# Seven products of halves in place of eight in the down projection of six blocks

## The chip, the cores and the metric

The kernel runs on one core of a Trainium2 chip. The time is that of the device, in microseconds (us), from start to end of one execution. One execution is also taken by the hardware profiler; the rows below come from it. Engines: PE is TensorE (matmuls; PEld is its weight load), DVE is VectorE, ACT is ScalarE, POOL is GpSimd, SP is SyncE, whose queue issues nearly all DMAs here. L74 is line 74 of the kernel, the helper through which all matmuls go, so matmuls are told apart by the names of their tiles.

## The reference

One transformer block on `x` of 4 x 1024 x 512 in float32. `x` is normalized to `xn`; a linear attention with decay (16 heads of 32, chunks of 128, ternary weights) and a gated feed-forward are both computed from `xn`, and both are added to `x`:

```python
xn = _layernorm(x)
gate = jnp.einsum('bsd,hd->bsh', xn, w_gate)      # 2048 hidden
up   = jnp.einsum('bsd,hd->bsh', xn, w_up)
gated = jax.nn.silu(gate) * up
ffn  = jnp.einsum('bsh,dh->bsd', gated, w_down)   # the down product
x = x + attention(xn, ...) + ffn
```

The change is to the last product, `gated` (tokens x 2048) by `w_down` (2048 x 512).

## The kernel before

**Blocks and stages.** The 4096 tokens are worked off in eight blocks of 512 (`b` is 0 to 7 in the code; the text counts blocks 1 to 8). The 2048 hidden units are 16 tiles `j` of 128. A block's feed-forward has two halves `hh` of eight tiles. For each tile, `ffn_up` makes the gate and up products (two stages of 12 matmuls of 512 columns into a bank `psf`), ACT applies silu (L693), DVE multiplies by the up product (L696), and the float32 result is split into two float16 tiles: ACT casts the high half (L699), POOL or DVE subtracts it for the low half (L700). Both lie in a tile `ghl`, of which there are eight. After eight tiles, `ffn_down` makes the down product: for each of four groups of 128 tokens, 8 tiles times 3 matmuls of 512 columns (high by high, high by low, low by high), 96 matmuls per half, and DVE adds the bank to `acc` (L720). `acc` holds `x` at the start and goes out by DMA when its last part is in.

**Weights.** Block 1 scales the weights by powers of two, splits them in two float16 halves and keeps them: gate and up in DRAM (`gu_d`, loaded again per block in 512 KB pieces `gu`, four buffers), down in SBUF (`wd`, all of it). In block 1 the down product follows two tiles at a time; from block 2 on it runs as above.

**Attention.** It is cut in halves of 256 tokens. `att_half` is a generator of some 27 steps: q, k (staged through DRAM into `qst` and `kst`), v, then scores into a single bank `pss`, multiplied by the mask on DVE (L545), split by ACT and POOL (L547, L548), products with v into `psa`, state, norms, and the projection (`turn`, `proj`). PSUM has three banks `psf`, four `psa`, one `pss`.

**Order.** One step of attention follows each stage of the feed-forward. The list `at` says in which step each half starts, `mh` when its input `h` is made; a block has 48 steps (32 up stages and 16 pieces of the down product), the program 384. TensorE keeps this order. The instructions of the other engines and of SP's queue are put in order by the scheduler when the program is built; each queue then runs in that order. Within an engine an instruction that waits holds up all behind it.

```python
    at = [round(36 + 22.4 * n) for n in range(2 * NB - 2)]
    at += [at[-1] + 14, at[-1] + 28]
```

Of the kernel before, what the change touches and what calls it, by code (L numbers as in the profile page):

```python
# [28 lines left out]
def block_kernel(ctx, tc, x, qkv_w, qkv_nwT, proj_w, proj_nwT, proj_nw, norm_w, s, w_gu, w_down, out):  # L29
# [73 lines left out]
    gu_d = dram.tile([P, NJ * 2048], F16, tag="gu_d", name="gu_d")  # L103
    wqkT = ct([P, CC, 2 * C], F16, "wqkT")
    wvT = ct([P, CC, C], F16, "wvT")
    wpT = ct([P, CC, C], F16, "wpT")
    wd = ct([P, NJ, 2, C], F16, "wd")
# [173 lines left out]
    raw, gu0, gq, lg = {}, {}, {}, [None]  # L281

    def raw_pair(g, kind):

        if kind == 2:
            return [t32(), t32()]
        if g == 0 and kind == 0:
            t = wt([P, 2, C], F32, "kn", 1)
            return [t[:, 0, :], t[:, 1, :], t]
        return [wt([P, C], F32, *(("ghl", 8) if g % 2 else ("xin", 4) if g else ("xn2", 2))) for _ in range(2)]  # L290
# [29 lines left out]
    def group_scale(g, kinds=(0, 1, 2)):  # L320
# [9 lines left out]
        if 0 in kinds:  # L330
            inverse(ug[:, gs], o[:, 0:1], 1 / XS)
            V.tensor_scalar(bsc0[:, gs], o[:, 0:1], 2.0**-30 / XS, None, ALU.mult)
# [9 lines left out]
    def group_conv(g, r, kinds=(0, 1, 2)):  # L342
# [3 lines left out]
        for kind in kinds:  # L346
# [3 lines left out]
            else:  # L350
                hi, lo = (wd[:, j, n, :] for n in range(2))
# [329 lines left out]
    def ffn_up(b, j, gu, bs, gts, E):  # L681
        xT = blk[b][0]
        xhi, xlo = xT[:, 0], xT[:, 1]
        pg = []
        for kind in range(2):
# [8 lines left out]
            else:  # L694
# [3 lines left out]
                ghl = wt([P, 2, HB], F16, "ghl", 8)  # L698
                A.copy(ghl[:, 0, :], gf)  # L699
                E.tensor_tensor(ghl[:, 1, :], gf, ghl[:, 0, :], ALU.subtract)  # L700
                gts.append(ghl)
            yield

    def ffn_down(b, k, js, gts, c):
        tsl = slice(k * P, (k + 1) * P)
        pd = bank(ps_f)
        for n, j in enumerate(js):
            gh, gl = gts[n][:, 0, tsl], gts[n][:, 1, tsl]
            T.matmul(pd, gh, wd[:, j, 0, :], start=(n == 0), stop=False)
            T.matmul(pd, gh, wd[:, j, 1, :], start=False, stop=False)  # L710
            T.matmul(pd, gl, wd[:, j, 0, :], start=False, stop=(n == len(js) - 1))
            if n % 4 == 3:
                if n == len(js) - 1:
                    add_acc(b * 4 + k, pd, c)
                yield
        if len(js) % 4:
            add_acc(b * 4 + k, pd, c)

    def add_acc(g, ps, c):
        V.scalar_tensor_tensor(acc[g], ps, c, acc[g], ALU.mult, ALU.add)  # L720
        parts[g] -= 1
        if parts[g] == 0:
            SY.dma_start(of[g * P : (g + 1) * P, :], acc.pop(g))

    def load_acc(b):
        for k in range(4):
            acc[4 * b + k] = load_x(4 * b + k, "acc", 8)
            parts[4 * b + k] = 1 + (2 if b else NG)

    def ffn(b):  # L730
        for hh in range(2):
            js = range(hh * NJ // 2, (hh + 1) * NJ // 2)
            gts = []
            for j in js:
                gu = wt([P, 2, 2, CC, P], F16, "gu", 4)
                SY.dma_start(gu.rearrange("p a b c d -> p (a b c d)"), gu_d[:, j * 2048 : (j + 1) * 2048])
                yield from ffn_up(b, j, gu, bsc, gts, V if j > js[-4] else G)
# [192 lines left out]
```

## Time and profile before

| | |
|---|---|
| median of 3 runs | 1368.39 us (1367.6 to 1370.64) |
| the profiled execution | 1368.61 us, its span 1366.7 us |
| granted TensorE clock, mean | 0.994 |
| busy: PE, DVE, ACT, POOL | 1322.6, 719.9, 550.3, 619.6 us |
| down matmuls (`psf<-wd,ghl`, 512 columns) | 1536, busy 352.3 us |
| gate and up matmuls (`psf<-xT,gu`, 512 columns) | 3072, busy 703.4 us |
| DMA: moved, busy share of queue 1 | 178.11 MB, 47.0% |

Busy time of a group counts only time in which no earlier matmul is still running; the mean duration of a matmul in the profile (380 ns) is longer than its spacing in a dense stream, since matmuls are pipelined. Spacing is read from start to start in the timeline. A group's row ends with the idle time of its engine ahead of it and what ended it; a row of the waits is engine, tile, line, what it waited for, us in total, times, longest.

### The profile page before, as it was taken

The page shows a single profiled execution, that of the slowest core. Times are in us where ns is not written, and L with a number is a line of the kernel's source. Part 1 is how long each engine was busy: PE and PEld are TensorE (multiplying, and loading weights), DVE is VectorE, ACT ScalarE, POOL GpSimd, SP SyncE. Part 2 cuts the span into 40 slices and gives each one's busy share as a digit, 9 for nine tenths or more (in the row PEclk, how much of TensorE's full clock was granted, in tenths as well). Part 3 has the DMA queues.
Part 4 walks back from the last instruction along what each step waited for, and adds up shares of the span by engine and source line. Part 5 has one row for each costly group of instructions (what it writes and reads, how often), then busy time and mean ns, then how long its engine had stood idle before and what let it go on. Part 6 is the DMA issues. An engine that isn't in the chain of part 4 may idle for free.

```text
span 1366.7 us, 21760 instructions
## 1 busy us (share of the span) xinstructions
PE 1322.6 (97%) x8514; PEld 695.6 (51%) x8514; DVE 719.9 (53%) x1415; ACT 550.3 (40%) x1033; POOL 619.6 (45%) x603
## 2 busy tenths in 40 slices
PE   5998989999999999999999999999999999999998
PEld 2443445554555545455455545555555555565554
DVE  7897764445544354453644446453553445356444
ACT  6754443343433334333334243342424334244341
POOL 3657672444624254353634246342545245255451
PEclk9999999999999999999999999999999999999999
DMA  9833836146261554426363354626283444535420
GB/s 343 294 124 114 231 101 180 48 137 156 87 191 31 165 128 125 140 59 173 94 155 108 103 141 104 178 69 162 80 181 95 116 116 106 142 109 124 105 66 31
DMA packets 155974, 178.11 MB, mean 130 GB/s; under 512 B 101600, under 2 KB 101600, under 8 KB 155872
## 3 DMA queue, kind: packets, MB, share of 16 engines
q1 hardware_dynamic: 155728, 176.73, 47.0%
q8 instruction: 66, 1.08, 0.3%
q14 instruction: 36, 0.29, 0.1%
q10 hardware_dynamic: 144, 0.01, 0.0%
HBM read 119.55 MB, written 33.55 MB: 112 GB/s over the span
## 4 chain that ended last, share of the span: by engine, by line
PE 79%; DVE 7%; POOL 7%; issue 3%; DMA 3%; ACT 1%; SPq 0%; POOLq 0%; ACTq 0%; DVEq 0%
PE psf L74 58%; PE psa L74 19%; PE pss L74 2%; DMA xin<-in_x_dram 2%; DMA xT<-xn 1%; POOL t L548 1%; DVE acc L720 1%; POOL xn L437 1%; DVE t L696 1%; DVE gs L312 1%; POOL rs L396 1%; POOL wd L360 1%; DVE t L239 0%; POOL ghl L700 0%; POOL gu L360 0%
## 5 line engine op out<-in xcount | busy, mean ns | idle before, releaser
L74 PE MATMUL psf<-xT,gu 128*128 128x512 f16 x3072 | 703.4, 381 | 10.6 <-POOL gu L360 5.5
L74 PEld LDWEIGHTS <-gu 128*128 128x128 f16 x3072 | 294.7, 98 | 338.0 <-issue 10.1
L74 PE MATMUL psf<-wd,ghl 128*128 128x512 f16 x1536 | 352.3, 380 | 2.7 <-ACT t L693 1.1
L74 PEld LDWEIGHTS <-ghl 128*128 128x128 f16 x1536 | 146.9, 98 | 164.3 <-issue 3.3
L548 POOL TENSOR_TENSOR t<-t,t 128x512 f16<-128x512 f32 x128 | 149.5, 1168 | 164.2 <-ACT t L547 163.9
L700 POOL TENSOR_TENSOR ghl<-t,ghl 128x512 f16<-128x512 f32 x86 | 102.6, 1193 | 163.4 <-ACT ghl L699 150.2
L696 DVE SCALAR_TENSOR_TENSOR t<-psf,bsc,t 128x512 f32<-128x512 f32 x128 | 95.9, 749 | 121.2 <-PE psf L74 104.8
L699 ACT CAST ghl<-t 128x512 f16<-128x512 f32 x128 | 79.0, 617 | 176.1 <-DVE t L696 175.6
L545 DVE SCALAR_TENSOR_TENSOR t<-pss,rs,mask 128x512 f32<-128x512 f32 x128 | 95.3, 744 | 77.2 <-PE pss L74 74.7
L693 ACT ACTIVATE t<-psf,ug 128x512 f32<-128x512 f32 x128 | 87.5, 684 | 98.0 <-PE psf L74 96.6
L74 PE MATMUL psa<-h,wqkT 128*128 128x256 f16 x1024 | 122.2, 273 | 0.0
L519 POOL TENSOR_TENSOR t<-t,t 128x512 f16<-128x512 f32 x28 | 32.6, 1163 | 195.3 <-ACT t L518 195.3
L547 ACT CAST t<-t 128x512 f16<-128x512 f32 x128 | 79.1, 618 | 101.9 <-DVE t L545 96.3
L74 PEld LDWEIGHTS <-wqkT 128*128 128x128 f16 x1024 | 99.7, 98 | 23.4
L720 DVE SCALAR_TENSOR_TENSOR acc<-psf,c,acc 128x512 f32<-128x512 f32 x56 | 41.8, 747 | 63.0 <-PE psf L74 62.7
L74 PEld LDWEIGHTS <-t 128*128 128x128 f16 x1040 | 47.6, 97 | 35.0 <-POOL t L548 3.4
L74 PE MATMUL psa<-wvT,h 128*128 128x512 f16 x256 | 60.5, 379 | 0.0
L74 PE MATMUL pss<-qst,kst 96*128 96x128 f16 x512 | 49.2, 218 | 8.7 <-DVE t L545 6.5
L74 PE MATMUL psa<-wpT,vhl 128*128 128x512 f16 x240 | 56.7, 379 | 0.0
L620 POOL TENSOR_TENSOR vhl<-t,vhl 128x512 f16<-128x512 f32 x30 | 34.7, 1155 | 48.0 <-ACT vhl L619 48.0
L573 POOL TENSOR_TENSOR t<-t,t 128x512 f32<-128x512 f32 x28 | 36.1, 1288 | 44.1 <-DVE t L572 18.6
L508 DVE SCALAR_TENSOR_TENSOR vhl<-psa,rs,vhl 128x512 f16<-128x512 f32 x32 | 24.0, 749 | 56.2 <-ACT vhl L507 54.5
(188 smaller groups left out, 1340.8 us busy)
## 6 DMA issues: line engine op xcount, KB each, us to landing
gu<-gu_d SPq DMA_DIRECT2D x112, 512.0 KB, 3.6
qst<-sd SPq DMA_DIRECT2D x48, 256.0 KB, 4.8
kst<-sd SPq DMA_DIRECT2D x48, 256.0 KB, 4.7
xin<-in_x_dram SPq DMA_DIRECT2D x32, 256.0 KB, 3.0
acc<-in_x_dram SPq DMA_DIRECT2D x32, 256.0 KB, 2.8
gu_d<-gu SPq DMA_DIRECT2D x16, 512.0 KB, 4.1
sd<-qhl SPq DMA_DIRECT2D x16, 512.0 KB, 2.6
sd<-khl SPq DMA_DIRECT2D x16, 512.0 KB, 3.3
```

What stands on the lines that cost most here:

```text
L74: tc.keep_in_program_order(nc.tensor.matmul(*a, **k))
L519: G.tensor_tensor(vrl, vr, vrh, ALU.subtract)
L545: V.scalar_tensor_tensor(sm, pss, u.rk, mask[:, 4 * qd : 4 * qd + 4, :], ALU.mult, ALU.mult)
L547: A.copy(u.smh, sm)
L548: G.tensor_tensor(u.sml, sm, u.smh, ALU.subtract)
L573: G.tensor_tensor(u.o, u.o, oc, ALU.add)
L620: G.tensor_tensor(on[:, 1, :], u.o3, on[:, 0, :], ALU.subtract)
L693: pa = A.activation(sl, pm, AF.Silu, scale=ug[:, j // 2 : j // 2 + 1])
L696: pv = V.scalar_tensor_tensor(gf, pm, bs[:, j // 2 : j // 2 + 1], sl, ALU.mult, ALU.mult)
L699: A.copy(ghl[:, 0, :], gf)
L700: E.tensor_tensor(ghl[:, 1, :], gf, ghl[:, 0, :], ALU.subtract)
L720: V.scalar_tensor_tensor(acc[g], ps, c, acc[g], ALU.mult, ALU.add)
```

## The change

In blocks 3 to 8 the down product of each half is taken as a 2 x 2 product of halves: tokens in two halves of 256 (T), hidden tiles in pairs of even and odd (the contraction), outputs in two halves of 256 columns (F). Seven products of sums of these take the place of eight products of parts (Strassen's scheme in the form with shared sums). Each of the seven is 2 groups of 128 tokens by 4 pairs by 3 matmuls, 24 matmuls of 256 columns.

- **Sums of the activations** are made as the tiles appear (`summed`): per pair POOL makes four sums of 128 x 256; two stand in the tile itself, three quarters go to a tile `ss`. Casts and low halves follow. The plain operands lie in `ghl` (now four tiles of a pair), the sums in `wda`.
- **Sums of the weights** are made once, beside block 2 (`down_sums`): for each of 8 groups a load of `w_down`, four sums on POOL, casts on ACT, low halves on DVE, and stores to a DRAM tile `wd_d`, which also gets copies of the three plain quarters that are used.
- `wd` is no longer one tile: the weights of block 1 and 2 lie in four `wda` and four `wdb` tiles. From block 3 on, the `wdb` tiles take the weights of the products from DRAM, seven loads of 512 KB per half, four ahead of the products and three as buffers come free; `wda` holds the sums of the activations.
- **Accumulation:** four banks of sums go to `acc` by nine DVE operations of 128 x 512 per half, in place of four; `acc` is now a tile for 256 tokens.
- **Order:** blocks 3 to 8 have 46 steps (14 down steps in place of 16), the program 372. `at` keeps 22.4 steps up to the fifth half and takes 21.5 after it. `bsc0` is smaller by 2^-2, for the range of the sums. In blocks 3 to 8 DVE takes the low halves of the last two tiles of a half, before those of the last three.

```diff
-    wd = ct([P, NJ, 2, C], F16, "wd")
+    wd_d = dram.tile([P, 2, 7, NJ // 4, 2, UT], F16, tag="wd_d", name="wd_d")
...
+    def wd_tile(hh, shape=(P, 2, 2, C)):
+        return wt(list(shape), F16, "wdb" if hh else "wda", 4)
...
+    def summed(ops, late):
+        g0 = []
+        def split(dst, src, E):
+            src = src.rearrange("p (a t) -> p a t", t=UT)
+            A.copy(dst[:, :, 0, :], src)
+            E.tensor_tensor(dst[:, :, 1, :], src, dst[:, :, 0, :], ALU.subtract)
+        def done(j, gf):
+            E = V if j > late else G
+            if j % 2 == 0:
+                ops.append((wt([P, 4, 2, UT], F16, "ghl", 4), wd_tile(0, (P, 4, 2, UT))))
+                g0[:] = [gf]
+                G.tensor_tensor(gf[:, UT:], gf[:, :UT], gf[:, UT:], ALU.subtract)
+                split(ops[-1][0][:, :2], gf, E)
+            else:
+                ss = wt([P, 2 * C], F32, "ss", 1)
+                f0 = g0[0]
+                G.tensor_tensor(ss[:, :UT], gf[:, UT:], f0[:, UT:], ALU.subtract)
+                G.tensor_tensor(ss[:, UT : 2 * UT], ss[:, :UT], f0[:, :UT], ALU.add)
+                split(ops[-1][0][:, 2:], gf, E)
+                split(ops[-1][1][:, :2], ss[:, : 2 * UT], V)
+                G.tensor_tensor(ss[:, 2 * UT : 3 * UT], gf[:, :UT], ss[:, :UT], ALU.subtract)
+                split(ops[-1][1][:, 2:3], ss[:, 2 * UT : 3 * UT], V)
+        return done
...
+    SEVEN = (
+        (("a", 0), 0, 0, ((0, 0),)),
+        (("a", 1), 4, 1, ((1, 1),)),
+        (("s", 1), 3, 2, ((1, 1),)),
+        (("s", 0), 6, 0, ((0, 1), (1, 0), (1, 1))),
+        (("a", 3), 5, 1, ((1, 0),)),
+        (("s", 2), 2, 2, ((0, 1),)),
+        (("a", 2), 1, 3, ((0, 0),)),
+    )
+    def load_seven(hh, n):
+        w = wd_tile(1, (P, NJ // 4, 2, UT))
+        SY.dma_start(w, wd_d[:, hh, SEVEN[n][1]])
+        return w
+    def ffn_seven(b, ws, ops, hh):
...
+            for k in range(2):
+                ks = slice(k * P, (k + 1) * P)
+                for i, o in enumerate(ops):
+                    gh, gl = (o[op[0] == "s"][:, op[1], m, ks] for m in range(2))
+                    for a, m, first in ((gh, 0, fresh and k + i == 0), (gh, 1, False), (gl, 0, False)):
+                        stop = last and i == len(ops) - 1 and a is gl
+                        T.matmul(pd[:, k, :], a, w[:, i, m, :], start=first, stop=stop, skip_group_check=True)
+            for th, fh in quarters:
+                a = acc[b * 2 + th][:, :, fh * UT : (fh + 1) * UT]
+                V.scalar_tensor_tensor(a, pd, c, a, ALU.mult, ALU.add)
...
+            if n + 4 < len(SEVEN):
+                ws.append(load_seven(hh, n + 4))
+            yield
+    def down_sums(g):
+        hh, i = divmod(g, NG // 2)
+        w = wt([P, 2, 2, UT], F32, "ss", 1)
+        SY.dma_start(w, w_down[2 * g * P : 2 * g * P + 2 * P, :].rearrange("(r p) (f q) -> p r f q", p=P, q=UT))
...
+            G.tensor_tensor(w[:, r, f, :], w[:, ra, fa, :], w[:, rb, fb, :], ALU.subtract)
...
+            A.activation(t[:, :, 0, :], w[:, r], AF.Copy, scale=o)
+            V.scalar_tensor_tensor(t[:, :, 1, :], w[:, r], o, t[:, :, 0, :], ALU.mult, ALU.subtract)
+            SY.dma_start(wd_d[:, hh, 3 + 2 * r : 5 + 2 * r, i].rearrange("p f n q -> p f (n q)"), t.rearrange("p f n q -> p f (n q)"))
+        for r in range(2):
+            SY.dma_start(wd_d[:, hh, r, i], wd[g][:, r, :, :UT])
+        SY.dma_start(wd_d[:, hh, 2, i], wd[g][:, 1, :, UT:])
...
+                if b > 1 and j - js[0] in (2, 3, 4, 5):
+                    ws.append(load_seven(hh, j - js[0] - 2))
...
-    TS = 48
-    at = [round(36 + 22.4 * n) for n in range(2 * NB - 2)]
+    steps = [48, 48] + [46] * (NB - 2)
+    t0 = [sum(steps[:b]) for b in range(NB)]
+    at = [round(36 + 22.4 * min(n, 4) + 21.5 * max(n - 4, 0)) for n in range(2 * NB - 2)]
...
+            if b == 1 and i % 5 == 2 and i // 5 < NG:
+                down_sums(i // 5)
```

## The prediction

> **What bounds the kernel now.** I read the page's first part and its groups, then the busy times of the middle blocks, then what TensorE waited for.
>
> ```profile
> PE 1322.6 (97%) x8514; PEld 695.6 (51%) x8514; DVE 719.9 (53%) x1415; ACT 550.3 (40%) x1033; POOL 619.6 (45%) x603
> ...
> L74 PE MATMUL psf<-wd,ghl 128*128 128x512 f16 x1536 | 352.3, 380 | 2.7 <-ACT t L693 1.1
> ...
> L548 POOL TENSOR_TENSOR t<-t,t 128x512 f16<-128x512 f32 x128 | 149.5, 1168 | 164.2 <-ACT t L547 163.9
> ```
>
> ```profile
> 830.00:995.00 165.00, 164.29 (x1094) 86.70 (x1092) 81.76 (x163) 62.74 (x115) 74.69 (x74) 1.00 0.45 122
> 995.00:1160.00 165.00, 165.00 (x1079) 88.03 (x1076) 77.75 (x154) 63.22 (x118) 70.99 (x72) 1.00 0.49 121
> 840.00:850.00 10.00, 10.00 (x57) 5.37 (x55) 7.92 (x19) 3.85 (x8) 9.10 (x11) 1.00 0.18 54
> ```
>
> Columns after the stretch: PE, PEld, DVE, ACT, POOL busy, granted clock, DMA share, GB/s. TensorE has no idle time in a middle block, at full clock; the other engines have half the time free. In the last row POOL is busy 9.1 of 10 us and TensorE still never waits. In all of 340 to 1340 us TensorE is idle 9.5 us, and the list of its waits there is short:
>
> ```profile
> PE pss L74 <- DVE t L545: 4.5, 5, 1.2
> PE psa L74 <- DVE Sst L594: 2.2, 1, 2.2
> PE psa L74 <- POOL t L548: 1.0, 2, 0.6
> ```
>
> So TensorE's work sets the time from block 2 on, and every us taken from it counts, until another engine's answer comes later than TensorE asks for it.
>
> **The TensorE work.** The down products of blocks 3 to 8 are 6 x 2 x 96 = 1152 matmuls of 512 columns. They become 6 x 2 x 7 x 24 = 2016 of 256 columns: 7/8 of the columns, in 1.75 times as many instructions with a weight load each. The price of each form, from the timeline of TensorE:
>
> ```profile
> 837.89 0.83 PE L74 MATMUL psa<-t,kn 128*128 128x128 f16 x12
> 838.57 2.75 PE L74 MATMUL psf<-wd,ghl 128*128 128x512 f16 x12
> ...
> 842.88 2.75 PE L74 MATMUL psf<-wd,ghl 128*128 128x512 f16 x12
> 845.47 1.91 PE L74 MATMUL psa<-h,wqkT 128*128 128x256 f16 x16
> 847.22 2.75 PE L74 MATMUL psf<-wd,ghl 128*128 128x512 f16 x12
> ```
>
> From start to next start, twelve 512-wide matmuls take 2.59 us (216 ns each), sixteen 256-wide ones with a weight load each 1.75 us (109.4 ns), twelve 128-wide ones 0.68 us (57 ns). A weight load alone lasts 98 ns, yet at 128 columns the stream is not slower than its columns. A rule speaks against the change here: the Trainium skill, "TensorE: Matmul & The Clock Gate", under "The mechanism", says that a weight load overlaps a running matmul only where their row groups differ, and all of these use all rows. By it a 256-wide step would cost 98+109 = 207 ns and a 512-wide one 314: 2016 x 207 = 417 us against 1152 x 314 = 362, a loss of 55 us. The rows show the loads hidden, so I take the rows: 1152 x 216 = 248.8, 2016 x 109.4 = 220.6, **28.2 us less**, on the engine that sets the end.
>
> **What is added beside it.** Per half of a block (four pairs of hidden tiles):
> - POOL: four 128x256 subtractions or additions a pair, 16 in all, and one split (`late` is one tile later, 1.17 us) that DVE did before. No 256-wide POOL row exists in f32. Half of the 1.29 us row (L573) is 0.64, the whole is 1.29; the 128x4 rows take 0.26 to 0.34, so a fixed part of 0.26 plus half of the rest is 0.78. I take 0.75: 12 + 1.2 = 13.2 us.
> - DVE: four splits of 128x512 (0.69) and four of 128x256 (0.42, the L563 row), nine accumulations of 0.75 in place of four, one split less: 2.8 + 1.7 + 3.7 - 0.7 = 7.5 us.
> - ACT: four casts of 0.62 and four of 0.37: 4.0 us.
>
> A block of about 160 us then holds POOL 72 + 26 = 98 us (61%), DVE 80 + 15 = 95 (59%), ACT 71 (44%). On average they stay beside TensorE's work. Locally it is tighter. In a stretch of four steps with scores and a pair (some 12.2 us of TensorE: four times 2.59 and about 0.45 of attention) POOL has four score splits, two `ghl` splits and four half-width sums: 6 x 1.17 + 4 x 0.75 = 10.0 us, 82% where it was 57%. Where a chunk's norms (two passes of 1.29, two powers of 0.55, the state's 1.07, a split of 1.16: 5.9 us) fall in the same stretch, POOL passes 100% and has to catch up in the next product stage. As `at` packs halves closer (21.5 steps against 22.4) while blocks are 46 steps, attention moves to the up products in blocks 5 to 8, where the sums are made; there the two coincide. What is queued behind a sum on POOL is the low half of the scores (L548 before), which TensorE wants two steps, 6 us, after the score matmuls; PSUM, DVE, ACT and POOL need 0.2+0.75+0.62+1.17 and about 0.4 of handing on, 3.1 us, so some 3 us of queue is free. The single score bank gives DVE's mask product about 2 us of slack per step.
>
> A second rule weighs on this:
>
> ```profile
> L700 DVE TENSOR_TENSOR ghl<-t,ghl x42: 676/693/1810, 220.2 to 1338.8; 128x512 f16<-128x512 f32 x42
> ```
>
> Most take 0.69 us, the worst 1.81 beside a POOL operation; the page's mean is 848 ns. The Trainium skill, "SBUF — State Buffer", "Who interferes with whom", has a DVE operation with two SBUF inputs and a reading GpSimd one exclude each other for the whole instruction. It agrees in kind. For the 8 new splits of a half the row says 8 x 0.16 = 1.3 us; the rule's worst, a whole POOL operation each, 9.4 us. POOL will be busier, so I put 2 us on DVE and POOL, off TensorE's path until a queue is late.
>
> TensorE's idle time of 9.5 us in 1000 is 0.75 us per half. With POOL's load up by 40% I take 0.7 us more per half, **+8 us** over twelve; from 0 (the 9.1-of-10 row) to 30 (2.5 us per half, if the crowded stretches of blocks 5 to 8 cost 4 us each).
>
> **Start of the seven products.** The last pair's sums run, after its last matmul: DVE 0.2+0.75, POOL twice 0.75, ACT 0.62, DVE 0.69 twice in its queue, handing on 0.4: 4.9 us. The third product is the first to read them, for its fourth operand: 2 x 2.6 + 9 x 0.11 = 6.2 us. Slack 1.3 us, more with attention between; inside the 0 to 30.
>
> **Weights from DRAM.** 84 loads of 512 KB (44 MB, on 178 MB) go through SP's queue. Each of the last three of a half waits for a product and is wanted three products, 7.8 us, later; the `gu` loads of this size land in 3.6. The first four of the next half wait on SP too, and behind them stand staging stores of q and k and transposes; but both sides follow TensorE's order, so I charge no queueing. Contention remains:
>
> ```profile
> 870.66 1.48 SPq L487 DMA_DIRECT2D kst<-sd  x3
> ```
>
> The median landing is 4.7 us, so about 876.8; the scores that read it start at 878.36. Slack is 1.5 us there and 3 to 6 in most halves; one 512 KB load in between costs up to 3. Taken in the 0.7 per half; at worst 1.5 us in each of 12.
>
> **Block 2's weight sums and block 1.** Eight times: one 512 KB load, four POOL sums (3 us), two casts, two splits, five stores, three of them of 512-byte pieces. The issue order puts these on SP among block 1's loads and block 2's transposes, and on POOL mostly between attention halves (POOL idle at 220 to 230 us). `ln` of block 3 takes the `xn2` buffers after the last stores. Cover: POOL and DVE at about half load. If it fails, what waits is the conversion stream of block 1, whose stalls (27 us idle by 170 us) could go either way: -4 to +8, **+2**.
>
> **Tail.** The last half starts 25 steps before the end (372-347) and not 29 (384-355), so the final transposes and projection come after the last product:
>
> ```profile
> 1350.04 0.60 PE L78 MATMUL psa<-ident,t 128*128 128x128 f32 x4
> ...
> 1350.68 0.59 ACT L634 CAST t<-psa 128x512 f16<-128x512 f32 x1 [8.21 <-PE psa L78]
> ...
> 1351.30 0.69 DVE L635 TENSOR_TENSOR t<-psa,t 128x512 f16<-128x512 f32 x1 [0.30 <-ACT t L634]
> ```
>
> The cast and the low half, 1.3 us and 0.2 of handing on, were under products and are now bare: **+1.5**.
>
> Sum on the profiled execution's 1368.6 us (span 1366.7; the median of the runs shown is 1368.4, the same): -28.2 + 8 + 2 + 1.5 = -16.7, **1352 us**. About 0.2%, 2.7 us, is what a measurement of this kernel tells from no change.
>
> **Rivals.**
> - *Late halves bound by POOL.* Attention and sums coincide in blocks 5 to 8, eight halves; 2.5 us of stall each and 0.7 in the other four make 23 in place of 8: 1367, at best 1361. For it: 10.0 of 12.2 us before norms. Against: the 840 to 850 row, and product stages with almost nothing on POOL to catch up in.
> - *Slower: the in-order queues.* DVE's splits of the sums wait for ACT, that for POOL, and the next mask product stands behind them, with one score bank. There are 8 score steps in each of 12 halves, 96. From (28.2-3.5)/96 = 0.26 us each it decides against the change; at 0.5 us each, 48 us: 1392; at 0.35, 1378. For it: TensorE's longest list of waits is already on this product. Against: only 5 waits in 1000 us, and the issue order puts the splits two steps after their sums.
> - *Gain in full*: no added stall, 1344 to 1345, with block 1 kinder 1340.
>
> **How the numbers follow.** Forecast (1346 to 1359) 0.44, full gain 0.12, POOL-bound 0.23 (a quarter of it within 0.2%), in-order queues 0.21 (most of it slower by over 0.2%, a little same). Faster 0.72, same 0.08, slower 0.20. The range for 8 in 10, 1339 to 1379, reaches from block 1's best into the slower case.
>
> **What would show it.** Right: 256-wide products at 109 ns; POOL near 61% in blocks 3 to 8; TensorE idle under 20 us from 340 us on. Wrong: 256-wide products clearly over 109 ns; `pss` or `psa` matmuls waiting on DVE or POOL for tens of us; `wdb` or `kst` named as a releaser; block 2 starting more than 8 us later.

## The result, and the profile after

The change makes the kernel slower: 1385.8 us (median of 4 runs, 1384.4 to 1387.3) against 1368.0 for the kernel before; the ratio is 1.0128, 95% interval 1.0109 to 1.0146. The profiled execution took 1384.4 us with a span of 1382.6, so 15.9 us more span than before. The page's first line, and the engines' shares of the chain that ended last (the work followed back from the last instruction, at each step to what released it):

```profile
PE 1308.6 (95%) x9378; PEld 783.1 (57%) x9378; DVE 879.3 (64%) x1575; ACT 596.4 (43%) x1145; POOL 810.8 (59%) x839
...
PE 60%; DVE 14%; POOL 11%; DMA 6%; ACT 4%; issue 3%; SPq 0%; DVEq 0%; POOLq 0%; ACTq 0%
```

The same chain before:

```profile
PE 79%; DVE 7%; POOL 7%; issue 3%; DMA 3%; ACT 1%; SPq 0%; POOLq 0%; ACTq 0%; DVEq 0%
```

TensorE is busy 14 us less, where 28 were counted, and idle 74.0 us in place of 44.1. From 374 to 1340 us POOL is busy 60% of the time and DVE 62%, close to the forecast (61 and 59%), yet a quarter of the chain now runs over them. What TensorE waits for over the whole execution, the mask product first as before has it (L545 there, L552 here), then after:

```profile
PE pss L74 <- DVE t L545: 6.5, 8, 1.2
```

```profile
PE pss L74 <- DVE t L552: 14.5, 9, 5.6
...
PE psa L74 <- DVE Sst L601: 6.8, 4, 3.9
PE psf L74 <- ACT wda L728: 5.7, 2, 4.1
PE psa L74 <- POOL t L555: 5.6, 8, 1.3
```

The new ones are few and long, not many and short. The stalls above 0.25 us add up to 9.4 us from 340 us on before and to 32.0 after, and from 200 to 340 us to 0.6 and 9.2. Three places show how one comes about.

*Block 2* (timeline; start, duration, engine, line, tiles, and in brackets the idle time ahead with what ended it). The weight sums stand in three queues at once:

```profile
253.16 0.72 POOL L820 TENSOR_TENSOR ss<-ss 128x256 f32<-128x256 f32 x1 [2.48 <-DMA ss<-in_w_down_dram]
...
256.46 0.75 DVE L825 SCALAR_TENSOR_TENSOR xn<-ss,om,xn 128x512 f16<-128x512 f32 x1 [3.46 <-ACT xn L824]
...
258.58 0.75 DVE L825 SCALAR_TENSOR_TENSOR xn<-ss,om,xn 128x512 f16<-128x512 f32 x1 [1.37 <-ACT xn L824]
259.25 0.74 DVE L552 SCALAR_TENSOR_TENSOR t<-pss,rs,mask 128x512 f32<-128x512 f32 x1
...
260.04 0.58 PE L74 MATMUL pss<-qst,kst 96*128 96x128 f16 x4 [5.64 <-DVE t L552]
```

DVE stands 3.46 and 1.37 us for ACT, ACT for POOL, POOL for a load; the mask product (L552), whose scores were there at 252, is behind them in DVE's queue.

*Statistics of the next block.* DVE stood 2.80 us, until 842.78, at a normalization statistic (L396) for the load of `x`, which SP had issued at 838.3 behind a load of weights and two transposes. The state's additions were queued behind it, and TensorE waited 3.86 us at 845.9:

```profile
842.78 0.69 DVE L396 BATCH_NORM_STATS2 st<-xin 128x6 f32<-128x512 f32 x1 [2.80 <-DMA xin<-in_x_dram]
...
849.72 0.57 PE L74 MATMUL psa<-Sst,qst 96*128 96x32 f16 x16 [3.86 <-DVE Sst L601]
```

At 508 us DVE stood so for 4.10 us, and TensorE waited 2.66 us at 512.

*Start of the seven.* The last up product of this half ended before 994. Its answer (L702) and the sums that follow:

```profile
995.36 0.27 DVE L614 TENSOR_SCALAR f<-sq,f 128x1 f32<-128x1 f32 x1 [2.14 <-ACT junk L607]
...
997.29 0.55 POOL L620 TENSOR_TENSOR f<-f,mhalf 128x1 f32<-128x1 f32 x1 [0.84 <-DVE f L619]
...
999.92 0.75 DVE L702 SCALAR_TENSOR_TENSOR t<-psf,bsc,t 128x512 f32<-128x512 f32 x1
...
1000.87 0.72 POOL L741 TENSOR_TENSOR ss<-t,t 128x256 f32<-128x256 f32 x1
...
1001.55 1.59 POOL L627 TENSOR_TENSOR vhl<-t,vhl 128x512 f16<-128x512 f32 x1
1003.12 1.48 POOL L592 TENSOR_TENSOR S<-S,lsm 32x512 f32<-32x512 f32 x1
1004.57 0.71 POOL L742 TENSOR_TENSOR ss<-ss,t 128x256 f32<-128x256 f32 x1
...
1005.99 1.33 PE L74 MATMUL psf<-wdb,wda 128*128 128x256 f16 x4 [4.12 <-ACT wda L728]
```

The norms of an attention half go to and fro between DVE, ACT and POOL, and L702 stands behind them for some 6 us; then POOL's sums stand behind a split and the state's product. The third of the seven waits 4.12 us. The first two ran through: they read nothing of the last tile.

**The clock.** A stall can cost more than its length. One-microsecond stretches (length, PE busy, PEld, DVE, ACT, POOL, granted clock, DMA share, GB/s):

```profile
1007.00:1008.00 1.00, 1.00 (x7) 0.69 (x6) 0.04 (x1) 0.00 (x0) 0.00 (x0) 0.50 1.79 191
1008.00:1009.00 1.00, 1.00 (x6) 0.72 (x5) 1.00 (x3) 0.00 (x0) 0.00 (x0) 0.50 0.71 151
1009.00:1010.00 1.00, 1.00 (x21) 0.84 (x19) 1.00 (x4) 0.00 (x0) 0.11 (x1) 0.50 0.01 3
1010.00:1011.00 1.00, 1.00 (x11) 0.78 (x8) 1.00 (x2) 0.00 (x0) 0.92 (x2) 0.70 0.57 70
1011.00:1012.00 1.00, 1.00 (x12) 0.89 (x10) 0.45 (x2) 0.00 (x0) 0.76 (x4) 1.00 0.70 221
```

The granted clock is the share of its full clock that TensorE was given. From 1003.8 us, within the stall, to 1010.6 it is half. Summed over all such stretches (PE busy times one less the granted clock) this takes 5.4 us before and 15.6 after: three episodes in which TensorE worked there, nine here, most about 3.4 us long.

The nine episodes start whole multiples of 3.413 us apart, to within 0.02 us over the whole execution, so the clock is decided on a grid of windows that does not follow the stalls. The window before each of the nine held at least 1.95 us of idle time; the full-clock windows that went unpunished (from 30 us on) held at most 1.92. So the idle time within one window counts, and not the length of a stall: the 2.66 us at 512 lie in one window, the 2.43 us at 206 are cut by a border, 1.85 in one window and 0.58 in the next, and went unpunished; two stalls of 1.32 and 1.07 us at 1083 share a window and were punished. Over all twenty traces the limit lies between 1.7 and 2.0 us. The Trainium skill, "TensorE: Matmul & The Clock Gate", "What's actually happening", has the free-running windows of 3413 ns and half clock after an idle one. The runs agree on the windows, but one need not be idle throughout: of the nine here only the two at 123 and 256 us were (3.36 and 3.41 us).

So a span splits into idle time, loss to the half clock, and the rest, TensorE's dense work. The table does this from one and the same matmul early in block 3 to the end, since blocks 1 and 2 have the old down product (the first number is the time at which that matmul's wait begins):

| kernel | up to there | from there on | idle | half clock | dense work |
|---|---|---|---|---|---|
| before | 362.1 | 1004.7 | 12.3 | 1.7 | 990.7 |
| after | 373.6 | 1009.0 | 34.9 | 8.9 | 965.3 |
| no sums (e14) | 364.9 | 976.5 | 12.3 | 1.7 | 962.5 |
| sums made, three in four not read (e17) | 364.6 | 995.1 | 28.8 | 1.7 | 964.6 |
| sums read, no weight sums (e18) | 365.3 | 1004.6 | 35.3 | 4.4 | 965.0 |

The saving is 25 to 28 us in all of them. What takes it back in after is 22.6 us of idle time, 7.2 us of half clock, and a start of block 3 that is 11.5 us later.

### The profile page after: what moved, and what is told of

Read it like the earlier page. It is cut to its first block, busy times and chain, and to the rows that moved or that the text cites. A ratio compares the mean times of both kernels' runs of the same rounds, so it can differ in the third digit from the quotient of the medians.

```text
span 1382.6 us, 24118 instructions
## 1 busy us (share of the span) xinstructions
PE 1308.6 (95%) x9378; PEld 783.1 (57%) x9378; DVE 879.3 (64%) x1575; ACT 596.4 (43%) x1145; POOL 810.8 (59%) x839
## 4 chain that ended last, share of the span: by engine, by line
PE 60%; DVE 14%; POOL 11%; DMA 6%; ACT 4%; issue 3%; SPq 0%; DVEq 0%; POOLq 0%; ACTq 0%
PE psf L74 43%; PE psa L74 16%; DMA xin<-in_x_dram 3%; POOL t L555 2%; DMA ss<-in_w_down_dram 2%; DMA xT<-xn 2%; DVE t L702 1%; PE pss L74 1%; POOL xn L444 1%; DVE t L552 1%; POOL ss L820 1%; DVE wda L729 1%; DVE h L463 1%; POOL ghl L729 1%; DVE st L396 1%
## 5 line engine op out<-in xcount | busy, mean ns | idle before, releaser
L555 POOL TENSOR_TENSOR t<-t,t 128x512 f16<-128x512 f32 x128 | 153.4, 1201 | 96.0 <-ACT t L554 94.0
L74 PE MATMUL psf<-wdb,ghl 128*128 128x256 f16 (+1 forms) x1344 | 183.0, 293 | 2.9 <-ACT ghl L728 1.3
L702 DVE SCALAR_TENSOR_TENSOR t<-psf,bsc,t 128x512 f32<-128x512 f32 x128 | 95.5, 746 | 63.0 <-PE psf L74 57.6
L729 DVE TENSOR_TENSOR wda<-ss,wda 128x512 f16<-128x512 f32 x96 | 104.3, 1110 | 39.2 <-ACT wda L728 38.4
L552 DVE SCALAR_TENSOR_TENSOR t<-pss,rs,mask 128x512 f32<-128x512 f32 x128 | 94.8, 740 | 34.6 <-PE pss L74 32.9
L74 PE MATMUL psf<-wdb,wda 128*128 128x256 f16 x864 | 105.8, 281 | 9.2 <-ACT wda L728 5.7
L802 DVE SCALAR_TENSOR_TENSOR acc<-psf,c,acc 128x512 f32<-128x512 f32 x108 | 78.5, 744 | 45.5 <-PE psf L74 45.0
L728 ACT CAST ghl<-t 128x512 f16<-128x512 f32 x96 | 59.2, 617 | 91.2 <-DVE t L702 47.6
L74 PEld LDWEIGHTS <-wda 128*128 128x128 f16 x864 | 85.1, 100 | 22.9 <-ACT wda L728 6.3
L729 POOL TENSOR_TENSOR ghl<-t,ghl 128x512 f16<-128x512 f32 x72 | 84.4, 1172 | 11.9 <-ACT ghl L728 11.9
L736 POOL TENSOR_TENSOR t<-t 128x256 f32<-128x256 f32 x48 | 36.4, 759 | 61.9 <-DVE t L702 53.8
L728 ACT CAST wda<-ss 128x512 f16<-128x512 f32 x96 | 47.8, 510 | 48.3 <-POOL ss L742 45.0
L741 POOL TENSOR_TENSOR ss<-t,t 128x256 f32<-128x256 f32 x48 | 37.3, 778 | 49.8 <-DVE t L702 45.4
```

Of the source, the lines that this page charges most:

```text
L74: tc.keep_in_program_order(nc.tensor.matmul(*a, **k))
L552: V.scalar_tensor_tensor(sm, pss, u.rk, mask[:, 4 * qd : 4 * qd + 4, :], ALU.mult, ALU.mult)
L555: G.tensor_tensor(u.sml, sm, u.smh, ALU.subtract)
L702: pv = V.scalar_tensor_tensor(gf, pm, bs[:, j // 2 : j // 2 + 1], sl, ALU.mult, ALU.mult)
L728: A.copy(dst[:, :, 0, :], src)
L729: E.tensor_tensor(dst[:, :, 1, :], src, dst[:, :, 0, :], ALU.subtract)
```

## The experiments

My theory after the two traces: the operations of the sums lie in the in-order queues of DVE, POOL and ACT ahead of what TensorE waits for. Rivals: TensorE waits for the sums themselves; the transfers and accumulations cost; POOL's load is the bound.

### What each part costs

**e1_no_act_sums.** `summed` without its four sums and their splits; the products that read sums read plain tiles. Of the edit, the line of the products:

```diff
...
-                    gh, gl = (o[op[0] == "s"][:, op[1], m, ks] for m in range(2))
+                    gh, gl = (o[0][:, op[1], m, ks] for m in range(2))
```

> Left out: the sums of the activations and their splits (16 sums on POOL, 8 casts on ACT, 8 low halves on DVE per half of a block in blocks 3 to 8); the products that read sums read plain tiles in their place, so the same 2016 matmuls of 256 columns run, with the same loads of weights, the same accumulations and the weight sums beside block 2. Theory A (TensorE's 28 us are there, and what eats them in blocks 3 to 8 are queues of DVE and POOL that the sums lengthen, with the cold clock that follows each stall; after: 32 us of gaps from 340 us on against 9, and about 9 us of cold clock): some 20 us of gaps and most of the cold clock go, 1358 to 1364 us, ratio to the kernel before 0.993 to 0.997. Rival B (the loss is in the transfers of weights, their places in SP's queue and the nine accumulations, which all stay here): over 1375. Rival C (the 256-wide stream is dearer than 109 ns over the whole run): also over 1375, with few gaps.

1365.6 us, ratio 0.9988 (0.9981 to 0.9994). B and C fall, but A expected 1364 at most: the stalls of the statistics stayed (4.30 us at 512.7, 3.77 at 845.0), and those of block 2.

**e2_no_weight_sums.** `down_sums` without load, sums and splits; of the edit, the stores that take their place:

```diff
...
-            SY.dma_start(wd_d[:, hh, 3 + 2 * r : 5 + 2 * r, i].rearrange("p f n q -> p f (n q)"), t.rearrange("p f n q -> p f (n q)"))
+            for f in range(2):
+                SY.dma_start(wd_d[:, hh, 3 + 2 * r + f, i], wd[g][:, r, :, f * UT : (f + 1) * UT])
```

> Left out: beside block 2 the load of w_down for sums, the four sums on POOL, the casts on ACT and low halves on DVE; in place of the sums, plain halves of the weights are stored to DRAM, so as many bytes are stored and the later blocks run as in after. Theory A (in block 2 DVE's low half of the weight sums waits for ACT, that for POOL, that for a late load, and the mask product stands behind: 9.2 us of new gaps from 200 to 260 us and about 2 of cold clock): 1385.8 - 11 = 1375 us, ratio 1.005; gaps from 200 to 260 us below 1 us. Rival D (block 2's gaps come from the stores and SP's queue): 1383 or more, gaps there stay at 6 us or more.

1381.1 us, 1.0096 (1.0079 to 1.0113): between the two. The gaps from 200 to 260 us are gone, as A said, but at 164 to 170 us TensorE now waits 4.9 us where it waited 2.5. A removed part moves the other instructions too, and the kernel gains 4.7 us where 11 were expected.

**e3_stats_pinned.** One line, so that DVE meets the statistics later:

```diff
-            V.bn_stats(st, xt)
+            with after(pin if b > 2 else ()): V.bn_stats(st, xt)
```

> The statistics of the normalization for blocks 4 to 8 are held back on DVE until the up product before their place in the program is done; nothing else changes, TensorE's order is the same. In after DVE stands at such an operation for 4.1 us at 508 us and 2.8 us at 840 us, waiting for the load of x, with the mask product and the state's additions queued behind, and TensorE then waits 2.7 and 3.9 us, with a cold clock after each (3 us together). Theory A: these two stalls go, 1385.8 - 8 = 1378 us (1374 to 1381), no wait of this operation for a DMA over 1 us. Rival E (the place where it waits is only where the delay shows: the accumulations and splits queued there are late anyway): 1383 to 1387. Below -: the statistics now lie beside up products, where sums are made, and stalls there grow: 1388 or more.

1382.5 us, 1.0101 (1.0086 to 1.0116). The stall at 512 is gone and that at 846 is 0.56 us; new ones of 2.55 at 453 and 2.38 at 1132 give more than half of the 8 us back.

**e14_no_sums.** e1, e2 and e3 in one.

> Left out: all sums of activations and of weights with their casts and low halves (plain tiles and plain halves of the weights stand in for them), and the statistics are held back as in e3. All 2016 matmuls of 256 columns, weight transfers, accumulations and the order of the steps stay. Theory A (24 us of TensorE's work are saved; the stalls come from the sums and from the statistics): block 3 starts as in e2 (the mark at 366 us, before 362), the stretch from there 987 - 11 = 976 us: 1344 us (1340 to 1352), ratio 0.980 to 0.989. Rival B (transfers, accumulations, queue order cost by themselves): 1360 or more.

1343.0 us, 0.981 (0.9796 to 0.9825): theory A, on the number. Its page against that of after:

```profile
PE 1299.5 (97%) x9378; PEld 781.8 (58%) x9378; DVE 750.5 (56%) x1463; ACT 550.8 (41%) x1033; POOL 631.9 (47%) x615
...
PE 87%; DVE 4%; POOL 4%; DMA 2%; issue 1%; ACT 1%; SPq 0%; POOLq 0%; DVEq 0%; ACTq 0%
```

All 84 loads of weights for the products, all nine accumulations per half and the new order of steps are in it. They cost nothing that can be seen: from block 3 on it takes 28.2 us less than before, with the same idle time and the same loss to the clock; the start of block 3 is 2.8 us later.

**e17_sums_unread** and **e18_sums_read.** e14 with the activations' sums made again; in e17 the products read `ghl` in place of `wda` (the line of e1), in e18 the sums. Of a pair's four sums one, and not two, stands in the tile itself: L736 overwrites half of the even tile with a difference, and the second product reads it. So e17 leaves three in four unread.

> Left out: the sums of weights (as in e2 and e14), and the products read plain tiles in place of sums; the activations' sums and their splits are all made, into tiles that nobody reads. Statistics held back as in e3 and e14. e14, the same without the activations' sums, takes 1343 us. Theory load (the operations lengthen the queues of DVE, ACT and POOL, and what TensorE waits for is the old work behind them): most of the cost of the sums is here: 1358 to 1370 us. Theory lateness (TensorE waits for the sums themselves): 1343 to 1350 us.

> Left out: the sums of weights alone; statistics held back. The activations' sums are made and read. From e2 and e3: 1385.8 - 4.7 - 3.3 = 1378 us if the two effects add. The difference to e17 is what the reading costs: by the theory of load 5 to 12 us (the start of the seven in the late halves, 6 to 8 us of waits for sums with their cold clock), by the theory of lateness over 25 us.

e17: 1361.5 us, 0.9939 (0.9923 to 0.9956). e18: 1371.6 us, 1.0023 (1.0014 to 1.0031). Making the sums costs 18.5 us, reading the three 10.1: load, with lateness second. The 18.5 us are idle time from block 3 on (28.8 us against 12.3), not clock (1.7 in both). In e17 most waits are for old work behind the new; only 2.4 us, at 1061, are for an even tile whose cast comes after its difference on POOL:

```profile
PE pss L74 <- DVE t L552: 7.9, 7, 2.4
PE psf L74 <- DVE t L702: 6.0, 4, 2.4
PE psa L74 <- POOL t L555: 5.7, 7, 1.4
```

In e18 the reading adds the third product's waits, again in the late halves, and two episodes of half clock behind them (from 987 and 1345 us):

```profile
PE psf L74 <- ACT wda L728: 5.6, 2, 4.0
...
PE psf L74 <- DVE wda L729: 1.7, 2, 1.1
```

The kernels form a ladder in which each step is one part: no sums 1343.0; activations' sums made +18.5; read +10.1; weight sums (e3 against e18) +10.9; statistics not held back (after against e3) +3.3; that is 1385.8. The steps depend on their order, though. Taken from after alone, the activations' sums are worth 20.2 us (e1) and not 28.6, the weight sums 4.7 (e2) and not 10.9; e18 came out 6 us under the sum of the single effects.

### Which load

**e11_sums_on_dve.** After, with the four sums of a pair on DVE, as here in all four lines of `summed`:

```diff
...
-                G.tensor_tensor(ss[:, :UT], gf[:, UT:], f0[:, UT:], ALU.subtract)
+                V.tensor_tensor(ss[:, :UT], gf[:, UT:], f0[:, UT:], ALU.subtract)
```

> The kernel after with the four sums of activations per pair on DVE in place of POOL (16 per half; 0.76 us each on POOL, an estimate of 0.42 us on DVE from the 128x256 rows there). POOL falls from 59% to about 49%, DVE rises from 64% to about 69%. The rival of the prediction, POOL bounds the late halves: the waits for POOL's low halves of scores and the chain at the start of the seven shorten, 1385.8 - 8 = 1378 or less. Theory A'' (what is late is DVE's queue, with the mask product and the up product's answer in it): DVE's queue gets longer at the same places, 1386 to 1396, and the mask product's waits grow above 14.5 us.

1392.2 us, 1.0164 (1.0142 to 1.0186); POOL falls from 59 to 48%, DVE rises from 64 to 69%. The waits for POOL's low halves of scores (L555) fall from 5.6 to 1.9 us, those for DVE's mask product rise from 14.5 to 18.4. So POOL's load alone was not the bound; the delay went along with the work. The groups tell something else. In after, then in e11 (busy, mean ns, idle ahead):

```profile
L729 DVE TENSOR_TENSOR wda<-ss,wda 128x512 f16<-128x512 f32 x48 | 60.5, 1261 | 37.8 <-ACT wda L728 37.4
...
L729 DVE TENSOR_TENSOR wda<-ss,wda 128x256 f16<-128x256 f32 x48 | 46.1, 960 | 1.4 <-ACT wda L728 1.0
...
L742 POOL TENSOR_TENSOR ss<-ss,t 128x256 f32<-128x256 f32 x48 | 37.9, 790 | 0.7
```

```profile
L742 DVE TENSOR_TENSOR ss<-ss,t 128x256 f32<-128x256 f32 x48 | 49.2, 1024 | 1.1
L729 DVE TENSOR_TENSOR wda<-ss,wda 128x512 f16<-128x512 f32 x48 | 34.9, 726 | 3.9 <-ACT wda L728 3.8
```

The low halves of the sums took 1261 ns on the mean and take 726 once POOL makes no sums beside them; on DVE a sum takes up to 1024 ns (the mean of L742) in place of the 420 that I expected. What this slowing costs TensorE is not shown: no run does the same work without it.

**e12_b_staged_dve.** The same on top of e10 (below).

> The kernel e10 with the sums of activations on DVE. Where the order is mended, the question is which engine's load is left: theory A'' (DVE): slower than e10 by 3 to 10 us; rival (POOL): faster than e10 by 3 us or more; neither: within 2 us of it.

1381.9 us, 1.0092 (1.0074 to 1.011), against 1381.6 of e10: by the expectation, neither engine's load is the one that is left.

### Whether order cures it

**e4_sums_last**, **e5_plain_first**, **e6_last_pair_last**, **e9_plain_first_b**: the order of `SEVEN`, after: a0 a1 s1 s0 a3 s2 a2 (a from `ghl`, s from `wda`). e4: a1 a3 a2 a0 s1 s0 s2; e5 and e6: a1 a0 a3 a2 s1 s0 s2; e9: a2 a1 a0 a3 s1 s0 s2. In e6 and e9 the first two products take pairs 0 to 2 first, then pair 3:

```diff
...
+            if n == 0:
+                part(0, (0, 1, 2))
+                yield
+                part(1, (0, 1, 2))
+                pd = part(0, (3,))
+            elif n == 1:
+                pd = part(1, (3,))
+            else:
+                pd = part(n, (0, 1, 2, 3))
```

> The seven products in another order: the four that read plain tiles first, the three that read sums last, so that the last pair's sums are wanted at the fifth product and not at the third, 5.2 us later. The same work in all. Theory A (the start of the seven: the last pair's up product, sums and splits come late in the queues of DVE and POOL; in after about 5 us of gaps at 1002, 2 at 1083, 3 at 1354 and the cold clock behind them, some 6 us): 1385.8 - 14 = 1372 us (1368 to 1378), no wait for the sums of activations over 1 us. Rival F (plain low halves are as late as the sums, since they stand in the same queues): at most 4 us better, 1382 or more, the same stalls moved to the wait for plain tiles.

> The four products of plain tiles first, the three of sums last, as in the run before it, but with one other product between any two that add to the same bank (there two in a row did, and each half's second product then waited for DVE's accumulation, 12 times, 14.8 us). Theory A (the start of the seven waits for whatever of the last pair is late; with the sums wanted at the fifth product that leaves the plain tile): the waits for the accumulation go and those for plain tiles stay, 7 to 9 us of gaps at 1003, 1083 and 1355 with their cold clock: no more than 4 us better than after, 1381 to 1386. Rival G (the sums alone are late): 1385.8 - 10 = 1376.

> The same order, and of the first two products the first three pairs of tiles are worked off before the last pair of either. In before the last tile of a half was wanted 21 matmuls of 512 columns (4.5 us) after the start of the down product; in after it is the tenth matmul of 256 (1.0 us); here it is the 37th (3.9 us). Theory A: the gaps at 1003, 1083 and 1355 fall from 7 to 9 us to under 3 and no cold clock follows them: 1385.8 - 12 = 1374 us (1370 to 1378). Rival H (the up product's answer itself is late, since DVE's queue is late there, and everything after it moves with it): gaps stay over 6 us, 1380 or more.

> Plain products first, the last pair last, as e6, but in an order (third, second, first, fourth plain tile, then the sums) in which no product adds to a bank that DVE has still to read: in e6 the third product came 0.65 us after the first one's end and went to the same bank, and the wait for the accumulation was 21.5 us over 11 halves. From block 3's start to the end after takes 1009.0 us, before 1004.7, e6 1016.0 (block 1 and 2 differ by some us from kernel to kernel with the same instructions, so this stretch is compared). Theory A (the order at the start of the seven costs after about 11 us of gaps and 6 of cold clock): 1016 - 20 = 996 us in the stretch, 1372 us in all. Rival B' (each cure moves the stall to the next product that wants DVE): 1004 or more, 1380 or more.

e4 1393.8 us, 1.0185 (1.0169 to 1.02); e5 1388.5, 1.0143 (1.0124 to 1.0162); e6 1396.5, 1.0201 (1.0185 to 1.0217); e9 1389.4, 1.0137 (1.0121 to 1.0154): none better than after. In e4 and e6 my own edit made a new wait, since a product went to a bank that DVE had still to read. The waits of e4, then of e6:

```profile
PE psf L74 <- DVE acc L802: 14.8, 12, 3.0
```

```profile
PE psf L74 <- DVE acc L817: 21.5, 11, 3.9
```

e5 and e9 are nearly free of that (2.5 us once in e5). e5 has no wait for sums left, but 7.0 us for plain tiles (L728 and L729 of `ghl`): at 1011 and 1363 the plain tile is as late as the sum, because L702 is; at 1090 it is the tile before the last. e9 gives the last pair 3.9 us and still waits 9.7 us for it. By the numbers rival B' stands in e9, H in part.

But these orders did not do what I had meant. `a0` and `a1` lie in the even tile of a pair, `a2` and `a3` in the odd one, so the last tile of a half is read first by the third product in after, e5 and e6 (6.2 us after the start of the seven), by the second in e4 (3.6 us) and by the first in e9 (3.9 us). No order asked for the last tile later than after does, and two asked for it earlier: that late answers at the start of the seven can't be cured by order is not shown.

**e7_defer_splits.** Casts and low halves of a pair's sums one tile later (those of the last pair ahead of the products):

```diff
...
         def done(j, gf):
+            with after(pin):
+                while wait:
+                    wait.pop(0)()
...
-                split(ops[-1][1][:, :2], ss[:, : 2 * UT], V)
+                wait.append(lambda d=ops[-1][1]: split(d[:, :2], ss[:, : 2 * UT], V))
```

> The casts and low halves of the sums of a pair are held back behind the next tile's up product (one tile, 5 us, later); the products' order is that of after. Theory A' (DVE takes a low half of a sum before ACT and POOL have made it, 2.5 us idle at 665 us and 3.8 at 802, with the mask product queued behind): the waits of the mask product for DVE fall from 14.5 us to 11 and those of the state by a little: 1381 to 1384. Rival I (DVE is late because it has too much to do, not because it stands): no change, 1384 to 1388, the same mask products late.

1393.7 us, 1.018 (1.0151 to 1.021): the mask product's waits are 17.3 us, not 11. A' falls. That fits rival I better, though it is slower than either expected.

**e8_all** and **e10_b_staged.** e8: e6, e7, e3 and the weight sums in stages. e10: e9, the stages, and the statistics behind one of the seven products. The stages (`down_sums` now yields before its sums and before its casts):

```diff
...
-            if b == 1 and i % 5 == 2 and i // 5 < NG:
-                down_sums(i // 5)
+            if b == 1 and i % 5 in (0, 2, 4):
+                if i % 5 == 0 and i // 5 < NG:
+                    dsum.append(down_sums(i // 5))
+                with after(pin):
+                    for d in list(dsum):
+                        next(d, 1)
```

> All of it in one: plain products first, the last pair last, the splits of sums held back, the statistics held back, and the weight sums beside block 2 cut in three stages two steps apart (load; the four sums on POOL; casts, low halves and stores), so that no engine stands for the stage before. Same work as after. Theory A (TensorE's saving of 24 to 25 us is there, the rest is the order in the queues and the cold clock behind it): gaps from 200 us on under 15 us (51 in after, 10 in before), 1385.8 - 30 = 1356 us (1350 to 1362), ratio to the kernel before 0.988 to 0.995. Rival B' (POOL and DVE at 60% are late somewhere whatever the order, and each cure moves the stall): 1368 to 1380.

> The kernel e9 with the weight sums beside block 2 in three stages two steps apart and each stage held behind the up product before it, and the statistics of the normalization held behind the third or fourth of the seven products. Theory A: block 3 starts 7 us earlier than in after (9.2 us of gaps in block 2 go to 2 or 3), and the stretch from there on is 4 us shorter than e9's: 1372 - 11 = 1361 us. Rival B': 1372 or more.

e8 1391.2 us, 1.0168 (1.0149 to 1.0186), with e6's wait in it (19.8 us), slower than either side expected. e10 1381.6 us, 1.0087 (1.0068 to 1.0106), far from 1361; it has e9's order in it, with the last tile wanted early (9.5 us of waits for `ghl` from 997 us on). The mask product's waits are down to 4.5 us, and another stands in their place, the transposes of the attention's output; the norms that they need stand on DVE behind the statistics that were moved there (four of them and the four normalizations, 754 to 764 us):

```profile
PE psa L74 <- DMA vhl<-vhl: 6.6, 2, 5.5
```

**e13_phase.** The starts of the attention halves alone:

```diff
-    at = [round(36 + 22.4 * min(n, 4) + 21.5 * max(n - 4, 0)) for n in range(2 * NB - 2)]
+    at = [round(36 + 22.4 * min(n, 4) + 21.5 * max(n - 4, 0)) if n < 8 else 204 + 23 * (n - 8) for n in range(2 * NB - 2)]
```

> After, with the starts of the attention halves alone changed: the ninth half starts 8 steps earlier (14 steps after the eighth), and from there on one starts every 23 steps, as long as a half of the feed-forward, so that from the ninth half on the norms lie 4 and 8 steps ahead of the start of the seven products and not within two steps of it; the last two starts stay. Theory N (the last up product's answer is late on DVE behind the norms): the stalls at 1003, 1083 and 1268 (8.4 us, and some 4 of cold clock) go, those at 1355 stay: 1385.8 - 12 = 1374 us (1371 to 1378). Rival L (load: DVE and POOL are late there whatever stands ahead): the start of the seven still stalls 2 us or more in those halves, 1382 or more; also the tight start of the ninth half may cost some us where it stands, near 670 to 700.

1383.1 us, 1.0098 (1.008 to 1.0116). The stalls at 1003 and 1083 shrink to 0.3 us and to nothing, so theory N is right about these two. But L's number came: the third product now waits 1.6 us at 847 and at 1174, the crowd at the ninth half costs 2.70 us at 788 (`qst`) and 1.92 at 875 (`kst`), and ACT's silu is late by 1.5 us in three halves. From block 3 on e13 takes 1004.6 us, 4.4 less than after, but it starts block 3 2.7 us later.

**e15_phase_mended**, **e16_phase_staged**: e13 with e3 and the stages, at other steps than in e8 and e10 (none of them at the start of block 2's down products); e15 has e9's order of products as well, e16 that of after.

```diff
...
+    DS = [0, 4, 8, 17, 21, 25, 29, 33]
```

> The new phase of e13; the order of products of e9, with the last pair last; the weight sums of block 2 in three stages, none of them at the start of block 2's down products; the statistics held back as in e3. Full work. Theory N with A: the stalls of the start of the seven, of block 2 and of the statistics go: 1356 to 1364 us, ratio 0.991 to 0.997. Rival B' (each cure moves the stall): 1370 or more.

> As e15, with the order of the seven products as in after. Where theory N holds, the sums are in time for the third product once the norms are out of the way, and the order of the products does not matter: within 3 us of e15. Where the sums are late by themselves: 5 us or more slower than e15.

1397.9 us, 1.0216 (1.0194 to 1.0239), and 1388.2 us, 1.0155 (1.012 to 1.0191): B' again, and the order of products costs 9.7 us where it was to help or not to matter. e15, with e9's order, waits 12.1 us for plain tiles (L728 and L729 of `ghl`); e16 waits 1.8 for these and 6.4 for sums. Part of the difference is thus the last tile that e9's order asks for early. Waits for POOL's low halves of scores are 11.5 and 11.7 us (5.6 in after), presumably because the scores were moved with the attention.

No kernel that does the whole work beats the one before; the nearest (e10, e12, e13) stay 0.9 to 1.0% above it.

## Why the prediction was wrong, step by step

Forecast were 1352 us, 16.7 less than before: -28.2 + 8 + 2 + 1.5. In the profiled executions the span grew by 15.9 us: -25.4 of dense work, +29.8 of idle time and half clock from block 3 on (the tail is in it), +11.5 before that.

- **TensorE's 28.2 us: right.** The products take 109 ns per matmul, the weight loads are hidden, and from block 3 on dense work falls by 28.2 us in e14 and by 25.4 in after. The rule on weight loads that spoke for a loss of 55 us was rightly overruled by the rows. Where the 3 us between after and e14 go is open.
- **Tail, 1.5 us: right.** The last projection waits 0.68 and 0.34 us.
- **Transfers at no charge: right.** e14 has the 84 loads and takes 1343 us.
- **"+8 us" of stalls in blocks 3 to 8: the step that failed.** It was read from an average: 60% of POOL and DVE, and one row with POOL at 9.1 of 10 us where TensorE did not wait. Measured from block 3 on, idle time rose by 22.6 us (12.3 to 34.9) and the loss to the half clock by 7.2 (1.7 to 8.9), 29.8 in all, at the upper bound of 30. The idle time is mostly that of making the sums (e17: 16.5 us over e14), which holds up older work in the queues. The half clock had no term in the prediction at all: a stall was priced at its length.
- **"Start of the seven", 1.3 us of slack: wrong.** It was worked out for the third product's sums with a free queue. L702 was 6 us late behind the norms, in just those halves where `at` brings both together. And a tile that no slack was worked out for is wanted sooner than before: the tile before the last, by the tenth matmul of the first product (1.0 us after its start). Before, eighteen matmuls of 512 columns came ahead of it (3.9 us). At 1083 two waits of 1.32 and 1.07 us are for this tile.
- **Block 2's weight sums, "+2": 4.7 (e2) to 10.9 us (e3 against e18).** Block 3 starts 11.5 us later than before, of which 2.8 stay without any sums (e14). "POOL and DVE at about half load" was no cover for an engine that stands at an instruction whose operand is not there, and what waited was not the conversion stream of block 1 but the mask product of block 2.
- **Contention, "2 us" per half on DVE and POOL: measured 5 on DVE.** (1261 - 690) x 48, (960 - 420) x 48 and (1043 - 690) x 24 ns are 62 us over twelve halves. The rule of the Trainium skill, "SBUF — State Buffer", "Who interferes with whom", whose worst was put at 9.4 us, deserved more weight than the old row with POOL less busy; e11 shows its size. How much of the 18.5 us for making sums is this slowing, and how much the number of operations, stays open.
- **The rivals.** The in-order queues came (0.21), in place of the forecast (0.44), but not as priced: not 0.26 us in each of 96 score steps, but nine waits of up to 5.6 us, and a few more at states, sums and plain tiles. That 1385.8 lies between the 1378 and the 1392 of that rival is therefore luck. POOL alone as the bound does not stand: e11.

## What to carry to other kernels

Work moved off the bound engine is free only if each piece finds its operands ready when its turn in an in-order queue comes; mean load does not say this, so list, for each consumer that TensorE waits for, what stands ahead of it in the queue and what that waits for. Price a stall with the clock behind it: where idle time within one window of 3.4 us came to some 2 us, it cost here about 1.7 us more. Ask of each new order which operand it wants first. And before believing an estimate of hidden work, run it unread: e17 differs from e18 in one line and shows two thirds of what the activations' sums cost.

## What was not expected of the hardware

- Half clock for 3.4 us after a window with some 2 us of idle time in it: a product of 24 matmuls from 850.13 to the next start took 4.29 us, where a warm one takes 2.62.
- DVE's low halves of sums at 1261 ns with POOL's sums beside them and 726 without (e11).
- Kernels with the same instructions up to block 3 reach the same place in it at 373.6 us (after), 376.7 (e4) and 379.9 (e5) in their profiled executions. TensorE's order is the same in all, but DVE and ACT start some instructions in another order. Differences of 3 to 6 us between kernels of this family say little without the traces.
